# Later transposes of the row maxima, two pairs of heads in turn, and a longer lead of the preparation over the attention

## The chip, the cores and the metric

The kernel runs on one core of one Trainium2 chip. The metric is the device time of one launch in microseconds (us), given as the median of several runs. Five engines of the core matter here: TensorE (PE, with its weight loads PEld), VectorE (DVE), ScalarE (ACT), GpSimd (POOL) and SyncE (SP), whose queue issues nearly all DMAs. The profiles and the traces come from one profiled execution.

## What is computed

One layer of a perceiver: cross attention of 512 queries over a context of 8192 rows (16 heads of 64, that is 8 pairs of heads), then a state space block with its gated network, then a mixture of 16 experts. Only the first part is touched by the change.

```python
def _L0_xattn_ref(Q, K, V, Wq, bq, Wk, bk, Wv, bv, Wo, bo):   # Q: 512 x 512, K = V: 8192 x 512
    q = (scale * (Q @ Wq + bq)).reshape(bs, q_len, NH, DM)      # NH 16, DM 64
    k = (K @ Wk + bk).reshape(bs, kv_len, NH, DM)
    v = (V @ Wv + bv).reshape(bs, kv_len, NH, DM)
    qk = jnp.einsum('nlhd,nshd->nhls', q, k)
    a = jax.nn.softmax(qk, axis=-1)
    o = jnp.einsum('nhls,nshd->nlhd', a, v).reshape(bs, q_len, NH * DM)
    return o @ Wo + bo
...
x = x + _L0_xattn_ref(_layernorm(x), ctx_1024, ctx_1024, ...)
x = x + _L0_attn_ref(_layernorm(x), ...)     # state space block and gated network
x = x + _L0_ffn_ref(_layernorm(x), ...)      # router, 16 experts, shared expert
```

## The kernel before

**Preparation in four passes.** Each of the `NPASS` = 4 passes prepares two pairs of heads. The context is cut into `NCH` = 16 chunks of 512 rows. For each chunk a pass projects K for its two pairs (`kproj_units`, lines L254 to L262) and V (`vproj_units`, two groups, L278 to L285). Each of these four groups fills one PSUM bank, is copied out by ACT (L261, L284), and its rounding error is kept by DVE (L262 `khl`, L285 `vs`), after which the bank is free. The banks come from `bank_j`, two of them while attention runs. A group is cut into four steps; after each the generator yields the nanoseconds that the step is taken to need (648).

**Row maxima as side work.** The softmax needs an upper bound for each row ahead of the attention. `smax_units` multiplies the queries with the chunk's K (L303, into the two banks `psx`), ACT copies the scores out (L308 `sf`), and DVE keeps a running maximum (L316 `runm`). When a pass is through, `maxrow_units` reduces the running maximum of each pair on DVE (two L324 and one L325, the result is `mx`), waits for some steps, transposes it on PE (L329 `ptm`, which takes a bank from `bank_j` as well), copies it on ACT (L331 `mrow`), and sends it by two small DMAs on SP (L333) into row 64 of the tile `qlm`, where the scores of the attention read it.

These generators stand in a list, `side`. The function `pump` takes one step from the first generator in the list. It is called after every second projection step (every fourth in the first pass), and after every one when the list has more than two entries. A step that yields 0 uses up its pump like any other. In the last pass nothing is left to project when the maxima are reduced: the side list is then pumped empty, and the planner counts `LAST / 10` = 800 ns for each of these pumps.

**Attention in 480 + 32 steps.** 16 units (8 pairs, two halves of the queries) have `NSTEP` = 32 steps each. A step has the scores of 256 rows (L367 with `qhh`, L368 with `qlm` and `kb`), exponentials on ACT (L375, and L377 in every even step), the difference of their two precisions on DVE (L379 in odd steps, L380), and the products with V (L397, L400 reads the tile of L380). The products of a step are issued two steps after its scores. At the end of a unit its output is transposed (`unit_end`, L418, also into a bank of `bank_j`).

**The order.** From the second pass on, PE, DVE and ACT work in the order of the program (`manual_schedule`). The planner lets the preparation run ahead by `LEAD` ns of its own counted time, and then spreads the rest evenly over `NFILL` = 378 attention steps: half of a step's share before the products with V, half after them.

```python
rate = ((NPASS - 1) * PASSN + LAST - LEAD) / NFILL
...
    cur = scores(u, m, loads[n // 4], sp, n > NFILL)
    advance(start + LEAD + (n + 0.5) * rate)
    ...
        drain()
    advance(start + LEAD + (n + 1.0) * rate)
```

When a pair's first unit starts (n = 128, 256 and 384 for the first pairs of passes two to four), an assertion in the program wants its maxima to have been issued. The first pass runs alone; its maxima are reduced and transposed within the lead of the second. After the attention of the first 15 units, the last unit and the rest of the layer (`tail`) follow.

Of the kernel before, what the change touches and what calls it, by code (L numbers as in the profile page):

```python
# [41 lines left out]
def perceiver_layer(ctx: ExitStack, tc: tile.TileContext, a: dict, out: bass.AP):  # L42
# [87 lines left out]
    def bank_j(shape, dtype, name):  # L130

        if jn[1]:
            jn[0] += 1
            if jn[0] % 3 == 0:
                return ps_o.tile(shape, dtype, name=name, tag="po1")
        return ps_j.tile(shape, dtype, name=name, tag="pj")
# [34 lines left out]
    def stage_w(src, n, tag, stage=("wst", 1), bufs=2):  # L171
        st = sb2.tile([P, NC4, n], F32, name=f"wst_{tag}", tag=stage[0], bufs=stage[1])
        nc.sync.dma_start(st, src)
        return lambda: split_w(st, n, tag, bufs)
# [8 lines left out]
    def load_w(*x, **k):  # L183
        return stage_w(*x, **k)()
# [4 lines left out]
    def first_norm():  # L189
        xn = sb2.tile([P, 4, DM], F32, name="xn", tag="runm0", bufs=1)  # L190
        layernorm(sb1, xn, x_sb, "ln0")
        transpose_split(xn, xTh, xTl)
        bo_bc = sb2.tile([P, DM], F32, name="bo_bc", tag="t2k", bufs=4)
        nc.sync.dma_start(bo_bc, a["bo"].to_broadcast((P, DM)))
        for i in range(4):
            nc.gpsimd.tensor_tensor(x_sb[:, i, :], x_sb[:, i, :], bo_bc, ALU.add)
# [9 lines left out]
    def qproj(p, w):  # L206
        wh, wl = w
        ps = bank_j([P, NQ], F32, f"psq{p}")
        mm3(ps, lambda i: wh[:, i, :], lambda i: wl[:, i, :], lambda i: xTh[:, i, :], lambda i: xTl[:, i, :], NC4)
        q32 = sb2.tile([P, NQ], F32, name="q32", tag="t2k", bufs=4)  # L210
        nc.scalar.activation(q32, ps, AF.Identity, bias=bq_sb[:, p : p + 1], scale=1.0 / WS)
        qh = sb2.tile([P, NQ], F16, name="qh", bufs=4)
        ql = sb2.tile([P, NQ], F16, name="ql", bufs=2)
        split_dve(qh, ql, q32)
        return qh, ql

    def qplace(p, qh, ql):
        qhh = qhhs[p % NQT]
        qlm = qlms[p % NQT]
        for hh in range(2):  # L220
            s = slice(hh * 64, hh * 64 + 64)
            nc.sync.dma_start(qhh[0:64, hh, :], qh[s])
            nc.sync.dma_start(qhh[64:128, hh, :], qh[s])
            nc.sync.dma_start(qlm[0:64, hh, :], ql[s])
        state[p]["q"] = qhh, qlm

    def ctx_first(c):
        t = []
        for j in (0, 2):
            u = sb3.tile([P, 2, 2, CH], F16, name="ctxc", tag="phl" if c % 2 else "ctxc", bufs=4)  # L230
            t.append(u)
            f = sb2.tile([P, 2, CH], F32, name="cf", tag="p32", bufs=3)
            nc.sync.dma_start(f, a["ctx"][c][:, j : j + 2])
            if j:
                nc.vector.tensor_copy(u[:, 0], f)
            else:
                nc.scalar.copy(u[:, 0], f)  # L237
            nc.vector.tensor_tensor(u[:, 1], f, u[:, 0], ALU.subtract)  # L238
            nc.sync.dma_start(ctx_d[c][:, j // 2], u)
        return t  # L240

    def ctx_load(c):
        t = []
        for j in range(2):
            u = sb3.tile([P, 2, 2, CH], F16, name="ctxc", tag="ctxc", bufs=4)
            nc.sync.dma_start(u, ctx_d[c][:, j])
            t.append(u)
        return t
# [70 lines left out]
    def maxrow_units(p, i, runm):  # L319
        runm = runm[i]  # L320
        qlm = state[p]["q"][1]
        m = sb2.tile([P, 2, 4], F32, name="mx")
        for w in (256, 128):
            nc.vector.tensor_tensor(runm[:, :, :, 0:w], runm[:, :, :, 0:w], runm[:, :, :, w : 2 * w], ALU.max)  # L324
        nc.vector.tensor_reduce(m.rearrange("p h q -> p q h"), runm[:, :, :, 0:128], axis=AX.X, op=ALU.max)  # L325
        for _ in range(3):
            yield 0
        pt = bank_j([P, P], F32, "ptm")
        nc.tensor.transpose(pt[0:8, :], m.rearrange("p h q -> p (h q)"), ident)  # L329
        r = sb2.tile([8, P], F16, name="mrow")  # L330
        nc.scalar.activation(r, pt[0:8, :], AF.Copy, bias=PSHIFT, scale=-1.0)  # L331
        for hh in range(2):
            nc.sync.dma_start(  # L333
                qlm[64:65, hh, :].rearrange("o (a b) -> o a b", b=P), r[hh * 4 : hh * 4 + 4, :]
            )
        state[p]["ready"] = True
        yield 300

    bcount = [0]

# [88 lines left out]
    def filler():  # L429
        side = []  # L430

        def pump():
            while side:
                u = next(side[0], None)
                if u is not None:
                    yield u
                    break
                side.pop(0)

        def pass_weights(g):  # L440
            pr = (2 * g, 2 * g + 1)
            out = []
            for src, n, tag, bufs in (
                (a["Wk"][pr[0]], P, "k", 4), (a["Wk"][pr[1]], P, "k", 4), (a["Wv"][g], 256, "v", 2),
                (a["Wq"][pr[0]], P, "q", 2), (a["Wq"][pr[1]], P, "q", 2),
            ):
                w = stage_w(src, n, tag, bufs=bufs)
                yield None
                out.append(w())
            yield out[0:2], out[2], out[3:5]  # L450

        nw = None
        for g in range(NPASS):
            pr = (2 * g, 2 * g + 1)
            if g == 0:
                wk0 = load_w(a["Wk"][0], P, "k", bufs=4)
                nct = ctx_first(0)
                wk = [wk0, load_w(a["Wk"][1], P, "k", ("p32", 3), bufs=4)]
                wv = load_w(a["Wv"][0], 256, "v", ("p32", 3))
                nc.sync.dma_start(x_sb, a["x"])  # L460
                wq = [load_w(a["Wq"][p], P, "q", ("t2k", 4)) for p in pr]
            else:
                wk, wv, wq = nw
                qh = [qproj(p, w) for p, w in zip(pr, wq)]
                yield 2 * 2592
            runm = [None, None]
            ks = [[None] * NCH for _ in pr]
            for c in range(NCH):
                if c == NCH - 7 and g < NPASS - 1:
                    nws = pass_weights(g + 1)  # L470
                if c >= NCH - 7 and g < NPASS - 1:
                    nw = next(nws, None) or nw
                ct = nct
                nxt = g * NCH + c + 1
                if nxt < NPASS * NCH:
                    nct = ctx_first(nxt) if nxt < NCH else ctx_load(nxt % NCH)
                gens = [kproj_units(p, c, ct, wk[i], ks[i]) for i, p in enumerate(pr)]
                gens += [vproj_units(g, c, ct, wv, j) for j in range(2)]
                k = 0
                for n, gen in enumerate(gens):  # L480
                    for u in gen:
                        yield u
                        k += 1
                        if k % (2 if g else 4) == 0 or len(side) > 2:
                            yield from pump()
                if g == 0 and c == 0:
                    first_norm()
                    qh = [qproj(p, w) for p, w in zip(pr, wq)]
                    yield 2 * 2592
                if c == 2:  # L490
                    for p, q in zip(pr, qh):
                        qplace(p, *q)
                side += [smax_units(c, i, qh[i][0], ks[i][c], runm, g == 0) for i in range(2)]
            side += [maxrow_units(p, i, runm) for i, p in enumerate(pr)]
            if g == NPASS - 1:
                while side:
                    yield from pump()
                    yield LAST / 10
            passes[0] = g + 1

    fill = filler()
    done = [0.0]

# [45 lines left out]

    units = [(p, h) for p in range(NPAIR) for h in range(2)]  # L550
    NLAST = len(units) - 1
    LEAD = 27500
    loads = {}

    def load(j):
# [9 lines left out]
    load(0)  # L565
    advance(start + LEAD)
    load(1)
    pend, enders, early = [], [], weight_prep()
    NFILL = 12 * NSTEP - 6
    rate = ((NPASS - 1) * PASSN + LAST - LEAD) / NFILL  # L570
    sp = (sb2, sb3, 3)
# [12 lines left out]
    for n in range(NLAST * NSTEP):  # L584
        u, m = units[n // NSTEP], n % NSTEP
# [4 lines left out]
        cur = scores(u, m, loads[n // 4], sp, n > NFILL)  # L590
        advance(start + LEAD + (n + 0.5) * rate)
        if enders and m == 4:
            for _ in enders.pop(0):
                pass
        while len(pend) > (2 if m == 2 else 1):
            drain()
        advance(start + LEAD + (n + 1.0) * rate)
        pend.append((u, m, cur))
# [14 lines left out]
    u = units[NLAST]  # L613
# [881 lines left out]
```

## Time and profile before

| what | value |
|---|---|
| median of 3 runs | 2570.77 us (2567.15 to 2572.27) |
| the profiled execution's own time | 2565.43 us |
| its span in the profile | 2563.7 us |
| granted TensorE clock, mean | 0.979 |
| busy: PE / DVE / ACT / POOL | 2361.3 / 2046.2 / 1947.5 / 73.8 us |
| first pass and the lead | to about 293 us |
| attention and preparation together | about 293 to 1592 us |
| attention alone, with the tail's start | about 1592 to 1867 us |
| the eight transposes L329 | 271.7 to 1592.2 us |

A row of the timeline gives the start, the duration, the engine, the line with the operation, what is written from what, and in brackets the idle time of the engine just before it and what ended that. A row of the windows gives the busy time of PE, PEld, DVE, ACT and POOL in a stretch, then the granted clock of PE, the share of the DMA engines and their GB/s. In the view of a tile, the rows under "its engine sat idle before it" tell for how long the engine that was to write the tile had been idle and what ended it.

### The profile page before, as it was taken

The numbers are of one execution on the slowest core, as the hardware profiler recorded it, in microseconds if no ns is written. First come the engines' busy times: TensorE is split into PE (matmuls) and PEld (weight loads), VectorE is DVE, ScalarE is ACT, GpSimd is POOL, SyncE is SP. The second block draws the span as 40 slices with busy tenths as digits, with TensorE's granted clock in tenths as the row PEclk, the third lists the DMA queues.
The fourth block names the chain that finished last, engine by engine and source line by source line (L and its number), as shares of the span: only waits on it lengthen the run. The fifth ranks groups of instructions, "written<-read, shape, count | busy, mean of one in ns | idle before, by whom it ended". The sixth has DMA issues, their size and how long they took to land. (4 is left out here: it accounts for less than half of the span.)

```text
span 2563.7 us, 56681 instructions
## 1 busy us (share of the span) xinstructions
PE 2361.3 (92%) x22958; PEld 1722.3 (67%) x22958; DVE 2046.2 (80%) x2378; ACT 1947.5 (76%) x3734; POOL 73.8 (3%) x77
## 2 busy tenths in 40 slices
PE   7999899999999999999999998998878678899896
PEld 3555577777666777766777776897756456577775
DVE  6776578888888888887888777998899999746685
ACT  5787788888878888877888888997958557434685
POOL 3000000000000000000000000000000000001112
PEclk9999999999999999999999999999999889999998
DMA  7983777787777787777778664777711212388897
GB/s 267 304 272 133 215 213 227 231 238 232 216 231 227 219 247 236 226 213 213 240 216 234 175 171 133 196 207 210 200 59 40 101 50 84 125 281 274 315 360 232
DMA packets 355199, 529.52 MB, mean 207 GB/s; under 512 B 28194, under 2 KB 221922, under 8 KB 354660
## 3 DMA queue, kind: packets, MB, share of 16 engines
q1 hardware_dynamic: 349156, 513.23, 65.7%
q0 software_dynamic: 3616, 8.66, 1.5%
q8 instruction: 182, 2.98, 0.5%
q10 hardware_dynamic: 2160, 3.95, 0.5%
q14 instruction: 85, 0.70, 0.1%
HBM read 396.65 MB, written 126.97 MB: 204 GB/s over the span
## 5 line engine op out<-in xcount | busy, mean ns | idle before, releaser
L380 DVE TENSOR_TENSOR phl<-p,phl 128x1024 f16<-128x1024 f32 x512 | 626.8, 1225 | 191.5 <-ACT phl L377 175.6
L375 ACT ACTIVATE p<-pss 128x512 f32<-128x512 f32 x1024 | 597.6, 622 | 112.1 <-issue 43.5
L308 ACT ACTIVATE sf<-psx 128x512 f16<-128x512 f32 x1024 | 558.6, 625 | 70.2 <-PE psx L303 69.5
L367 PE MATMUL pss<-qhh,k 128*128 128x256 f16 x2048 | 478.3, 274 | 14.1 <-ACT phl L377 11.9
L368 PE MATMUL pss<-qlm,kb 128*128 128x256 f16 x2048 | 477.1, 273 | 0.8 <-DMA v<-v_d 0.7
L316 DVE TENSOR_TENSOR runm<-runm,sf 128x2048 f16<-128x2048 f16 x240 | 292.4, 1220 | 51.4 <-ACT sf L308 51.3
L397 PE MATMUL po<-v,phl 128*128 128x130 f16 x4096 | 322.3, 220 | 3.9 <-DVE oq L410 3.4
L377 ACT ACTIVATE phl<-pss 128x512 f16<-128x512 f32 x512 | 312.8, 611 | 0.0
L397 PEld LDWEIGHTS <-phl 128*128 128x128 f16 x4096 | 270.5, 98 | 61.7 <-issue 15.3
L278 PE MATMUL psv<-wh_v,ctxc 128*128 128x256 f16 x1024 | 283.4, 277 | 7.3 <-ACT wh_v L179 3.2
L279 PE MATMUL psv<-wl_v,ctxc 128*128 128x256 f16 x1024 | 282.0, 275 | 1.1 <-DVE wl_v L180 1.1
L280 PE MATMUL psv<-wh_v,ctxc 128*128 128x256 f16 x1024 | 282.0, 275 | 0.0
L367 PEld LDWEIGHTS <-k 128*128 128x128 f16 x2048 | 200.3, 98 | 65.0 <-issue 20.0
L368 PEld LDWEIGHTS <-kb 128*128 128x128 f16 x2048 | 200.7, 98 | 52.1 <-issue 14.9
L303 PE MATMUL psx<-khl,qh 64*128 64x512 f16 x1024 | 208.1, 386 | 18.2 <-ACT sf L308 13.1
L929 PE MATMUL py<-hs,ident 128*128 128x256 f32 x512 | 141.2, 430 | 76.6 <-DVE hs L926 76.5
L400 PE MATMUL po<-v,phl 128*128 128x65 f16 x4096 | 208.2, 193 | 1.4 <-DVE phl L380 1.4
L254 PE MATMUL psk<-ctxc,wh_k 128*128 128x512 f16 x512 | 197.4, 386 | 10.8 <-ACT ctxc L237 9.0
L379 DVE CAST phl<-p 128x1024 f16<-128x1024 f32 x256 | 176.1, 688 | 30.8 <-ACT p L375 30.6
L255 PE MATMUL psk<-ctxc,wh_k 128*128 128x512 f16 x512 | 196.0, 383 | 0.9 <-DVE ctxc L238 0.9
L256 PE MATMUL psk<-ctxc,wl_k 128*128 128x512 f16 x512 | 195.9, 383 | 0.0
L929 PEld LDWEIGHTS py<-hs,ident 128*128 128x128 f32 x512 | 104.8, 213 | 108.3 <-DVE hs L926 90.9
(315 smaller groups left out, 3814.4 us busy)
## 6 DMA issues: line engine op xcount, KB each, us to landing
v<-v_d SPq DMA_DIRECT2D x128, 520.0 KB
k<-k_d SPq DMA_DIRECT2D x256, 256.0 KB
ctxc<-ctx_d SPq DMA_DIRECT2D x96, 512.0 KB
wef<-in_gu_dram SPq DMA_DIRECT2D x72, 512.0 KB
v_d<-vs SPq DMA_DIRECT2D x128, 260.0 KB
k_d<-khl SPq DMA_DIRECT2D x128, 256.0 KB
kb<-k_d SPq DMA_DIRECT2D x128, 256.0 KB
wpm<-w_d SPq DMA_DIRECT2D x48, 512.0 KB
```

The source lines that it names most:

```text
L278: nc.tensor.matmul(ps[:, t, :], lhsT=ct[i // 2][:, 0, i % 2, sl], rhs=wh[:, i, :], start=i == 0, stop=False)
L279: nc.tensor.matmul(ps[:, t, :], lhsT=ct[i // 2][:, 0, i % 2, sl], rhs=wl[:, i, :], start=False, stop=False)
L280: nc.tensor.matmul(ps[:, t, :], lhsT=ct[i // 2][:, 1, i % 2, sl], rhs=wh[:, i, :], start=False, stop=i == NC4 - 1)
L308: nc.scalar.activation(dst, ps, AF.Copy, scale=1.0 / (8.0 * WS))
L316: nc.vector.tensor_tensor(r, r, sf, ALU.max)
L367: nc.tensor.matmul(ps[:, hh], lhsT=k[:, hh, sl], rhs=qhh[:, hh, qs], start=True, stop=False)
L368: nc.tensor.matmul(ps[:, hh], lhsT=b[:, hh, sl], rhs=qlm[:, hh, qs], start=False, stop=True)
L375: nc.scalar.activation(p32[:, i], pss[i], AF.Exp, scale=sc)
L377: nc.scalar.activation(ph[:, i], pss[i], AF.Exp, scale=sc)
L380: nc.vector.tensor_tensor(pl, p32, ph, ALU.subtract)
L397: nc.tensor.matmul(o, lhsT=ph[:, i, hh, qs], rhs=vv, start=first, stop=False, **kw)
L929: nc.tensor.matmul(py[:, j, :], lhsT=ident, rhs=hs[:, n, 1:], start=k == 0, stop=False)
```

## The change

Three edits. In `maxrow_units` seven steps that yield 0, where there were three, stand between the reduction and the transpose. The two pairs of a pass enter the side list as one generator, `turns`, which takes a step from each of them in turn, where they stood one behind the other. `LEAD` is 36000 where it was 27500, and `rate`, which is worked out from it, goes from 1723.3 to 1700.8 ns for each step.

```diff
@@ maxrow_units
         nc.vector.tensor_reduce(m.rearrange("p h q -> p q h"), runm[:, :, :, 0:128], axis=AX.X, op=ALU.max)
-        for _ in range(3):
+        for _ in range(7):
             yield 0
         pt = bank_j([P, P], F32, "ptm")
@@ new
+    def turns(gens):
+
+        while gens:
+            for g in list(gens):
+                u = next(g, None)
+                if u is None:
+                    gens.remove(g)
+                else:
+                    yield u
@@ filler
-            side += [maxrow_units(p, i, runm) for i, p in enumerate(pr)]
+            side.append(turns([maxrow_units(p, i, runm) for i, p in enumerate(pr)]))
@@ perceiver_layer
-    LEAD = 27500
+    LEAD = 36000
```

## The prediction

> **What bounds the kernel now.** I read the engine shares of the page first, then busy time by stage, then the tile of the transposed maxima, and last the timelines around its eight transposes.
>
> ```profile
> PE 2361.3 (92%) x22958; PEld 1722.3 (67%) x22958; DVE 2046.2 (80%) x2378; ACT 1947.5 (76%) x3734; POOL 73.8 (3%) x77
> ```
>
> ```profile
> 293.00:1578.00 1285.00, 1257.85 (x13105) 911.65 (x13102) 1050.97 (x1250) 1074.08 (x2115) 0.10 (x1) 1.00 0.75 217
> 1578.00:1602.00 24.00, 15.99 (x226) 14.30 (x226) 20.59 (x22) 14.91 (x30) 2.65 (x5) 1.00 0.45 119
> ```
>
> The second fence is busy time by window (PE, PEld, DVE, ACT, POOL; clock; DMA). While attention and preparation run together, PE is busy 98%, so only its 27 us of idle time can be won. In the 24 us in which the last pass drains, PE is busy 67% and DVE 86%: there DVE sets the pace.
>
> ```profile
>   DVE mx L325: 21.4, 7
> ...
>   DVE vs L285: 12.6, 6
> ...
>   ACT mrow L331: 16.6, 8
> ```
>
> This is the tile ptm: what ended the idle time ahead of the transposes (weight load and matmul are both counted), and who waited. Two things hold a transpose: the reduction mx, or the bank it takes, which the DVE correction of an earlier projection (vs, khl) frees. The PE timeline has each stall in its brackets:
>
> ```profile
> 271.68 0.27 PE L329 MATMUL ptm<-ident,mx 128*8 128x128 f32 x1 [3.19 <-DVE khl L262]
> 278.97 0.27 PE L329 MATMUL ptm<-ident,mx 128*8 128x128 f32 x1 [0.77 <-DVE vs L285]
> 708.24 0.27 PE L329 MATMUL ptm<-ident,mx 128*8 128x128 f32 x1 [2.68 <-DVE vs L285]
> 1153.88 0.27 PE L329 MATMUL ptm<-ident,mx 128*8 128x128 f32 x1 [2.40 <-DVE vs L285]
> 1163.62 0.38 PE L329 MATMUL ptm<-ident,mx 128*8 128x128 f32 x1 [3.07 <-DVE mx L325]
> 1585.25 0.27 PE L329 MATMUL ptm<-ident,mx 128*8 128x128 f32 x1 [3.67 <-DVE mx L325]
> 1592.24 0.27 PE L329 MATMUL ptm<-ident,mx 128*8 128x128 f32 x1 [3.57 <-DVE mx L325]
> ```
>
> With 0.26 us at 716.85 that is 19.6 us. The cause is a block of 3.1 us on DVE per pair:
>
> ```profile
> 1580.86 1.22 DVE L380 TENSOR_TENSOR phl<-p,phl 128x1024 f16<-128x1024 f32 x1
> 1582.00 1.94 DVE L324 TENSOR_TENSOR runm<-runm 128x2048 f16<-128x2048 f16 x2
> 1583.98 1.22 DVE L325 TENSOR_REDUCE mx<-runm 128x8 f32<-128x1024 f16 x1
> 1585.11 1.22 DVE L380 TENSOR_TENSOR phl<-p,phl 128x1024 f16<-128x1024 f32 x1
> ```
>
> **A rule weighed: the clock after a stall.** Columns as above; the seventh is the granted clock.
>
> ```profile
> 709.00:713.00 4.00, 4.00 (x22) 2.56 (x20) 3.28 (x6) 1.80 (x3) 0.00 (x0) 0.57 0.51 172
> 1592.30:1596.00 3.70, 3.70 (x54) 3.46 (x55) 2.88 (x3) 2.74 (x6) 0.00 (x0) 1.00 0.08 17
> ```
>
> After the stall of 2.68 us the clock was halved for about 3.4 us (1.7 us lost); after that of 3.57 it stayed full. The windows after 3.19 (0.58) and 3.07 (0.51) show the drop too: three drops, 5.1 us. The Trainium skill, "TensorE: Matmul & The Clock Gate", Part 1 on the clock gate, has the clock halved after an idle window of about 3.4 us and calls that window free-running; its section on oscillation asks for no gaps over that. By its length alone, only the two drain stalls would drop (3.4 us before) and a drain stall after (1.7). I take the trace: three drops before, and after the change a drop at about half of the stalls of 2.7 us or more. The sum below is 6.4 us by the trace and 5.2 by the rule.
>
> **The change part by part.** It adds no arithmetic: the same 16 L324, 8 L325, 8 transposes, 8 copies L331 and 16 DMAs L333 stand in another order. POOL issues none of them. I followed the yields by hand. One pump takes one step from the front of the side list, so two pairs in turn with seven steps each put 14 pumps between a pair's reduction and its transpose, where three were. n is the attention step. Before: reductions at n=118, 121, transposes at 120, 122 (first joint pass); 248, 251 and 250, 252; drain 375, 377 and 376, 378. After: 116, 117 and 122, 123; 247, 248 and 253, 254; 375, 375 and 382, 382. In the alone stage the transposes come at 18.7 and 19.7 us of the planner's time instead of 9.0 and 13.8.
>
> So the cover of a transpose is ample, but two blocks of 3.1 us now follow closely on DVE, and the question is what is late next: corrections that free banks, or L380, which attention needs two steps later. In joint work the way from a score to its use is 2 steps of about 3.3 us plus half the filling, 7.4 us; four exponentials at 0.48 and L380 at 1.15 take 3.4. That leaves 4 us. In the drain two bare steps of 1.58 us leave nearly none.
>
> *Alone stage.* The correction of the second K group ends at 271.62 as now. The V group runs through to 269.6 and the next group needs that bank: wait 2.05. The second reduction pushes the V correction to 275.3, where the group after would start at 274.3: 1.05. The first transpose now falls 0.65 us into a group and needs the bank of the one just ended (about 1.5 us for ACT and DVE): 0.85. Sum 3.95 and 0.3 of clock, against 3.96 and 1.7: gain 1.4 (0 to 3).
>
> *First joint pass.* From the end of the scores of 116: L380 to 3.4, reduction to 6.5, weight preparation 0.7, cast and L380 to 9.0, reduction to 12.1, V correction 12.75. PE wants that bank at 9.95: wait 2.85. The first transpose then stands right between two groups, so the next group waits for exponentials, cast and mrow on ACT: 1.6. With half a clock drop 5.15, against 2.68+0.26+1.7=4.64: loss 0.5 (-2 to +2). The same working for the old order gave 2.45 where 2.68 was measured.
>
> *Second joint pass.* The groups lie differently: the V correction is done at 12.15, PE asks at 12.0, and neither transpose waits. 0.5 with clock, against 2.40+3.07+1.7=7.17: gain 6.7 (3 to 7).
>
> *Drain.* Reductions 1582.0 to 1585.1 and to 1588.2, then L380 of step 376 at 1589.4. PE stands 0.8 for a bank of scores, then 4.35 in that step's second half, then 0.25: 5.4 against 7.24. Steps 380 on run 2.0 earlier. But unit 384 uses the first of these maxima: transpose at 1595.6, behind four exponentials on ACT to 1597.75, mrow 1598.0, two DMAs on SP 1.3 (L333 took 1.21 to 1.34 for two), packets 0.7 to 3 later (seen after these issues): 1600 to 1601.7, where PE is ready at 1597.9. Before, that score waited for its K load until 1601.44. SP's loads for 384 are issued ahead of these DMAs and are not held up. Gain 0.9, half a clock drop 0.85: nothing (-3 to +3).
>
> *Lead.* 27.5 to 36 us takes 22.5 ns off the filling of each of 378 steps and puts 8.5 us ahead of attention. PE had no gap from 279 to 292 and 2% in joint work, so this is time moved; if ACT stood in for PE there, 2% of 8.5 us would be lost. The transposes stay six, three and two steps ahead of their units. The first attention step hits the table load (1.28) with more PE work between the two score maxima: the 2.51 stall at 297.69 becomes about 1.8, gain 0.7.
>
> *Side work later.* Some ten pumps of score maxima are caught up two to a step. Such pairs in an even step cost 0.48 (PE waiting for sf L308 at 614.48, 1035.92); I count three: loss 1.5 (0 to 4). *Unit ends.* The output transposes also take a bank: before, waits of 1.58, 0.55, 1.65 and 1.80 followed them; after, three have the order of the 1.80 one (n=36, 68, 100) and three nearly none: loss 0.4.
>
> Sum: 1.4 - 0.5 + 6.7 + 0 + 0.7 - 1.5 - 0.4 = 6.4 us off the profiled execution's 2565.43 (span 2563.7): 2559.0. That execution is 5.3 below the median 2570.77; off the median, 2564.4.
>
> **The rivals.**
> 1. *The stalls move one for one.* For: DVE has the same 25 us of reductions, and its queue is in order. Against: it was 82% busy in joint work, and the order of the second pass leaves PE covered. If the second pass also waits 4.5 to 5: gain 2, 2569.
> 2. *Slower: the doubled DVE block reaches attention at every pass.* Two reductions, 6.2 us at once, ahead of L380. It decides if the 4 us of slack in joint work are not there (ACT or DVE behind already). Then each of four places costs 6.2 and a clock drop of 1.7, and 384 waits 3 for its row: 34.7 against 24.7 now: 2581. For: the drain shows it. Against: behind a block L380 ended at 1154.96 for the step scored at 1150.44, whose second half ran on PE only at 1164.66.
> 3. *All covered.* The 24.7 us go entirely: 2546. Against: the drain, where DVE is the bound.
> 4. That the change doesn't do what it says: it does more, 14 pumps for seven. That is in the sum.
>
> **How the numbers follow.** A measurement here tells about 0.2% (5.1 us) from no change. Forecast 0.52 (0.40 faster, 0.12 within), rival 1 0.18 (0.13 within, 0.05 slower as the catch-up grows to 4 and the drain costs 3), rival 2 0.18 (0.16 slower, 0.02 within), rival 3 0.12. Faster 0.52, same 0.27, slower 0.21. The bounds added up reach from 15 gained to 6 lost, 2555 to 2577; with the 4 us by which runs lie below their median the range is 2551 to 2577, which leaves out most of rivals 2 and 3.
>
> **What would show it.** Right: the ptm tile with under 3 us of PE stall in all; new waits of 1 to 3 us for khl or vs ahead of L254, L278 near 270, 275 and n=117 to 122; in the drain a wait of 4 to 5 us at L400 for L380; a wait for qlm at 1598 to 1601. Wrong: L380 waits at n=118 or 249 (rival 2), or the same stalls in the second pass (rival 1).

## The result: slower by 0.2%, with the transposes' stalls gone

The changed kernel took 2576.01 us (median of 20 runs, 2568.99 to 2583.08), the kernel before 2571.27 us (20 runs beside it). The ratio is 1.0020, with a 95% interval of 1.0011 to 1.0029. The forecast was 6.4 us faster; it became 4.7 us slower.

The profiled execution of the changed kernel took 2581.91 us, 16.5 more than that of the kernel before, and this is more than the medians differ. Up to the first score of unit 12 (n=384), where every pass has been prepared, it is 7.3 us behind (1607.70 against 1600.44). The other 9.2 us lie behind that point, where the order is the same in both. Over the fourteen profiles this stretch takes between 962.8 and 972.5 us without following the edits (963.3 before, 972.5 after, but 964.0 and 965.0 in e3 and e4, and 970.7 and 971.5 in e5 and e8); its cause is open. What follows explains the part ahead of n=384.

The first fence is the row of engine shares on the page of the changed kernel, the second the busy time by window (columns as in the prediction) in the stages that answer to those shown of before:

```profile
PE 2376.7 (92%) x22958; PEld 1743.7 (68%) x22958; DVE 2048.3 (79%) x2378; ACT 1962.3 (76%) x3734; POOL 69.6 (3%) x77
```

```profile
302.00:1586.00 1284.00, 1251.05 (x13059) 920.87 (x13057) 1047.18 (x1245) 1082.91 (x2104) 0.10 (x1) 1.00 0.74 216
1586.00:1610.00 24.00, 17.93 (x227) 15.35 (x226) 21.65 (x22) 15.11 (x32) 2.65 (x5) 0.93 0.43 113
```

In the joint stage PE is idle for 33 us (1284.00 - 1251.05), where it was 27; in the drain for 6.1 us, where it was 8.0. In the changed kernel the lines behind `turns` have numbers ten higher: L375, L377, L380 and L400 of before are L385, L387, L390 and L410. The tile ptm shows that the transposes are not the reason:

```profile
  DVE khl L262: 2.1, 2
  PE ptm L329: 1.6, 2
...
  ACT mrow L331: 1.6, 2
```

The waits of 21.4 and 12.6 us for mx and vs are gone. The timeline of PE shows what stands in their place (all gaps of 0.9 us or more between 260 and 1610, without those ahead of L303 and the three of 1.80 at unit ends):

```profile
272.13 0.27 PE L278 MATMUL psv<-wh_v,ctxc 128*128 128x256 f16 x1 [1.88 <-DVE khl L262]
275.84 0.38 PE L254 MATMUL psk<-ctxc,wh_k 128*128 128x512 f16 x1 [0.93 <-DVE vs L285]
282.74 0.27 PE L329 MATMUL ptm<-ident,mx 128*8 128x128 f32 x1 [0.91 <-DVE khl L262]
...
713.30 0.38 PE L254 MATMUL psk<-ctxc,wh_k 128*128 128x512 f16 x1 [1.79 <-DVE vs L285]
...
1162.90 0.38 PE L254 MATMUL psk<-ctxc,wh_k 128*128 128x512 f16 x1 [0.99 <-DVE vs L285]
1181.18 0.27 PE L378 MATMUL pss<-qlm,kb 128*128 128x256 f16 x1 [1.65 <-DMA qlm<-mrow]
...
1597.85 0.62 PE L410 MATMUL po<-v,phl 128*128 128x65 f16 x8 [4.22 <-DVE phl L390]
1608.96 0.27 PE L378 MATMUL pss<-qlm,kb 128*128 128x256 f16 x1 [0.99 <-DMA qlm<-mrow]
```

But for the 1.65 us for qlm at 1181.18, these are waits of the kind that the prediction named. With smaller ones of 0.89, 0.38 and 0.27 us they come to 14.9 us where 19.6 went, so a part of the gain is left. The loss is at L303, the scores from which the row maxima are taken. First the group's row on the page of before, then on that of after (busy time, mean ns, idle time just before them):

```profile
L303 PE MATMUL psx<-khl,qh 64*128 64x512 f16 x1024 | 208.1, 386 | 18.2 <-ACT sf L308 13.1
```

```profile
L303 PE MATMUL psx<-khl,qh 64*128 64x512 f16 x1024 | 213.4, 385 | 27.9 <-ACT sf L308 20.4
```

Idle time rises by 9.7 us, and busy time by 5.3 for the same 1024 matmuls, since the second of two matmuls, when it waits for its bank, is counted in the group's span. And the waits recur:

```profile
794.59 0.86 PE L303 MATMUL psx<-khl,qh 64*128 64x512 f16 x2 [0.48 <-ACT sf L308]
848.51 0.86 PE L303 MATMUL psx<-khl,qh 64*128 64x512 f16 x2 [0.49 <-ACT sf L308]
902.96 0.86 PE L303 MATMUL psx<-khl,qh 64*128 64x512 f16 x2 [0.48 <-ACT sf L308]
956.88 0.86 PE L303 MATMUL psx<-khl,qh 64*128 64x512 f16 x2 [0.48 <-ACT sf L308]
```

They lie 54 us apart, that is 16 attention steps or two chunks of the preparation, through most of a pass. Elsewhere such a pair of matmuls takes 0.39 us with no gap ahead of it; here it takes 0.86 after a gap of 0.48. That is about 0.95 us each, or 1.03 by the count of the table below. Before, away from the maxima of a pass, such rows are few; beside these three there are two, at 1377.01 and 1431.15:

```profile
614.48 0.86 PE L303 MATMUL psx<-khl,qh 64*128 64x512 f16 x2 [0.49 <-ACT sf L308]
1035.92 0.86 PE L303 MATMUL psx<-khl,qh 64*128 64x512 f16 x2 [0.48 <-ACT sf L308]
1090.43 0.86 PE L303 MATMUL psx<-khl,qh 64*128 64x512 f16 x2 [0.49 <-ACT sf L308]
```

In the changed kernel, what PE waits for is on ACT at that time:

```profile
846.87 0.61 ACT L385 ACTIVATE p<-pss 128x512 f32<-128x512 f32 x1
847.34 0.62 ACT L387 ACTIVATE phl<-pss 128x512 f16<-128x512 f32 x1
847.82 2.18 ACT L308 ACTIVATE sf<-psx 128x512 f16<-128x512 f32 x4
```

ACT is through with the last of the step's four exponentials at about 847.9 and then copies four score banks in a row. Two pairs of scores came in one step with four exponentials, and there are two banks for them.

### The profile page after: what moved, and what is told of

Read it like the earlier page. It is cut to its first block, busy times and chain, and to the rows that moved or that the text cites. A ratio compares the mean times of both kernels' runs of the same rounds, so it can differ in the third digit from the quotient of the medians.

```text
span 2580.2 us, 56647 instructions
## 1 busy us (share of the span) xinstructions
PE 2376.7 (92%) x22958; PEld 1743.7 (68%) x22958; DVE 2048.3 (79%) x2378; ACT 1962.3 (76%) x3734; POOL 69.6 (3%) x77
## 5 line engine op out<-in xcount | busy, mean ns | idle before, releaser
L390 DVE TENSOR_TENSOR phl<-p,phl 128x1024 f16<-128x1024 f32 x512 | 626.3, 1225 | 186.1 <-ACT phl L387 167.3
L385 ACT ACTIVATE p<-pss 128x512 f32<-128x512 f32 x1024 | 593.9, 614 | 96.7 <-PE pss L378 58.8
L377 PE MATMUL pss<-qhh,k 128*128 128x256 f16 x2048 | 480.5, 275 | 13.8 <-ACT phl L387 10.4
L387 ACT ACTIVATE phl<-pss 128x512 f16<-128x512 f32 x512 | 312.4, 610 | 0.0
L377 PEld LDWEIGHTS <-k 128*128 128x128 f16 x2048 | 200.9, 98 | 71.4 <-issue 24.5
L303 PE MATMUL psx<-khl,qh 64*128 64x512 f16 x1024 | 213.4, 385 | 27.9 <-ACT sf L308 20.4
L410 PE MATMUL po<-v,phl 128*128 128x65 f16 x4096 | 208.3, 193 | 6.2 <-DVE phl L390 6.2
L939 PE MATMUL py<-hs,ident 128*128 128x256 f32 x512 | 149.0, 448 | 68.9 <-DVE hs L936 68.8
L939 PEld LDWEIGHTS py<-hs,ident 128*128 128x128 f32 x512 | 110.7, 224 | 103.0 <-DVE hs L936 81.5
## 6 DMA issues: line engine op xcount, KB each, us to landing
k<-k_d SPq DMA_DIRECT2D x256, 256.0 KB
k_d<-khl SPq DMA_DIRECT2D x128, 256.0 KB
kb<-k_d SPq DMA_DIRECT2D x128, 256.0 KB
```

The costliest lines, as they stand in the source:

```text
L377: nc.tensor.matmul(ps[:, hh], lhsT=k[:, hh, sl], rhs=qhh[:, hh, qs], start=True, stop=False)
L385: nc.scalar.activation(p32[:, i], pss[i], AF.Exp, scale=sc)
L387: nc.scalar.activation(ph[:, i], pss[i], AF.Exp, scale=sc)
L390: nc.vector.tensor_tensor(pl, p32, ph, ALU.subtract)
L939: nc.tensor.matmul(py[:, j, :], lhsT=ident, rhs=hs[:, n, 1:], start=k == 0, stop=False)
```

## The theory and its rivals

**Spacing (P).** A chunk counts 16x648+8x406 = 13616 ns for the planner. At LEAD 36000 the rate is 1700.8, so a chunk lasts 8.006 attention steps. At every second border between chunks two score maxima come one projection step apart instead of two, because an exhausted entry still counts when the side list is taken to be long (`len(side) > 2`). With 8.006 steps to a chunk this close pair falls at the same place for whole passes, and at LEAD 36000 that place is an even step, which has four exponentials, in the second and third of the three joint passes (n=142, 158 and so on; an odd step, n=11 to 91, in the first). At 27500 a chunk has 7.90 steps, and the pairs wander. By hand, 14 even steps hold two score maxima before and 22 after.

**Rivals.** The seven steps and turns delay the side work, and catching up costs (S, B). Or a longer lead costs, or helps, by itself (L).

The waits of all runs stand in one table. Each interval between two matmuls on PE, from the first projection of the second pass to the first score of n=384, is compared with the lower quartile of the intervals between the same two neighbours over all fourteen profiles; what lies above is added up for the matmul that came late. Intervals at the halved clock are added up apart. "All" is the length of this stretch in the one profiled execution. Even in order the columns are not zero (9.2 us for L400 and L397 before). The expectations below count fewer of the waits at L303 (16.6 us before and about 31 after), so only their differences can be set beside this column. The ratio is to the kernel before in the same session.

| run | even steps with two | all, us | L303 for sf | transposes | projections for banks | products with V | half clock | ratio |
|---|---|---|---|---|---|---|---|---|
| before | 14 | 1343.5 | 25.1 | 20.2 | 9.2 | 9.2 | 4.9 | 1 |
| after | 22 | 1350.3 | 41.8 | 1.1 | 15.9 | 13.2 | 1.5 | 1.0020 |
| e1: lead 36000 only | 19 | 1350.8 | 31.2 | 21.3 | 8.3 | 9.0 | 4.6 | 1.0011 |
| e2: steps, turns, lead 27500 | 15 | 1349.9 | 33.3 | 1.1 | 15.2 | 14.0 | 6.6 | 1.0015 |
| e3: after, lead 39000 | 8 | 1342.7 | 24.6 | 1.1 | 17.3 | 13.9 | 8.4 | 0.9985 |
| e4: after, one step later | 13 | 1343.0 | 30.6 | 1.7 | 19.2 | 12.5 | 3.5 | 0.9990 |
| e5: after, border | 10 | 1334.1 | 24.3 | 1.1 | 17.3 | 12.9 | 2.6 | 0.9945 |
| e6: before, lead 39000 | 8 | 1328.3 | 19.3 | 14.3 | 4.1 | 9.5 | 5.0 | 0.9920 |
| e7: e8, last pass in line | 7 | 1331.0 | 21.1 | 1.1 | 15.6 | 13.6 | 3.3 | 0.9905 |
| e8: after, 39000, border | 7 | 1331.8 | 21.1 | 1.1 | 15.6 | 13.8 | 3.9 | 0.9929 |
| e9: three, in line, 39000, border | 5 | 1322.8 | 15.6 | 14.7 | 4.1 | 9.3 | 3.3 | 0.9895 |
| e10: seven, in line, 39000, border | 11 | 1329.0 | 25.5 | 1.9 | 8.4 | 13.4 | 2.6 | 0.9912 |
| e11: three, in turn, 39000, border | 6 | 1323.4 | 17.4 | 4.9 | 8.1 | 13.1 | 3.4 | 0.9899 |
| e12: before, lead 42000 | 15 | 1346.4 | 27.0 | 19.9 | 8.1 | 9.2 | 6.0 | 1.0000 |

After less before: L303 +16.7, transposes -19.1, projections +6.7, products with V +4.0, half clock -3.4, waits for qlm +1.8 (not in the table), the rest 0.1: +6.8. By the same count the doubled even steps cost 1.2 us each after (26.5 us in 22), the doubled odd ones 0.6 (7.7 in 13).

## The experiments

### e1 and e2: the lead alone, the steps alone

e1 is the kernel before, e2 the changed kernel, each with one line edited.

```diff
-    LEAD = 27500
+    LEAD = 36000
```

> The kernel before, with LEAD 36000 alone (three steps, pairs one behind the other). Theory of the step (P): at LEAD 36000 a chunk of the preparation lasts 13616/1700.8 = 8.006 attention steps, so the two score maxima that stand close together at each chunk's border fall at the same place for whole passes, in a step with four exponentials. Followed by hand, 19 even steps have two score maxima in them, 14 before. The waits of PE for sf at L303 go from 16.6 us to about 21 to 25, the stalls of the eight transposes stay near 19 us: 2576 (2573 to 2581). Rival (S): the seven steps and the turns cause the waits, the lead is harmless: 2571, L303 waits 16 to 18 us.

Measured: 2573.77 us, ratio 1.0011 (1.0001 to 1.0021). L303 rose by 6.1 us and the transposes kept their stalls, as P expected; the time is 2.6 above the 2571.2 of before. So the lead alone costs, by little more than the noise.

```diff
-    LEAD = 36000
+    LEAD = 27500
```

> The changed kernel with LEAD put back to 27500 (seven steps and turns stay). P: 15 even steps with two score maxima, waits for sf at L303 about 18 us instead of 31; stalls of the transposes gone as in the changed kernel, but the rows for n=256 come only one step ahead, with a wait for qlm of 3 to 5 us there: 2566 (2562 to 2569). S: no better than the changed kernel, 2576.

Measured: 2574.85 us, ratio 1.0015 (1.0003 to 1.0026). P missed by 9 us. L303 stood at 33.3 us, 8.2 above before, though the even steps are nearly as many (15 and 14). So the seven steps and the turns have a cost at L303 of their own, beside the spacing at borders: the side work that comes later is caught up two to a step, and the larger waits at n=1, 130 and 258 (1.7 to 1.9 us each) stand at the start and in the steps after the maxima. S was right for this half. The wait for qlm at n=256 was 4.29 us, as expected. With the halved clock left out, the stretch of the table is 7.6 us longer in e1 than before, 4.7 in e2 and 10.2 in the changed kernel: both parts of the change cost.

### e3 and e4: the same kernel at another place of the pattern

e3 has LEAD 39000. e4 keeps the rate of the changed kernel and starts the attention one step later:

```diff
-    LEAD = 36000
+    LEAD = 37701
...
-    rate = ((NPASS - 1) * PASSN + LAST - LEAD) / NFILL
+    rate = ((NPASS - 1) * PASSN + LAST - 36000) / NFILL
```

> The changed kernel with LEAD 39000 (rate 1692.9, 8.04 steps to a chunk). P: by hand 8 even and 23 odd steps with two score maxima, where 36000 has 22 and 13. L303 waits about 15 to 18 us less than the changed kernel's 31: 2562 (2558 to 2566). S, and a rival (L) in which a longer lead costs by itself: 2576 to 2580.

> The changed kernel with the rate kept at 1700.8 and the lead longer by one attention step (37701): the same locked pattern, moved from even to odd steps. P: 13 even steps with two score maxima instead of 22, L303 waits down by 7 to 10 us: 2568 (2564 to 2571). L: 2577 or more. A resonance that costs in every phase: 2576.

Measured: e3 2567.37 us, ratio 0.9985 (0.9974 to 0.9996), L303 17.2 us below the changed kernel. e4 2569.19 us, ratio 0.9990 (0.9980 to 1.0000), L303 11.2 below. Both leads are longer than 36000 and both kernels are faster than at 36000, so a longer lead does not cost by itself. e4 has the same rate and the same locked pattern, moved by one step: from even to odd in the second and third joint pass, from odd to even in the first. So the parity of the step makes the difference. e3 missed its number by 5 us; in its profile banks and half clock took more than in the changed kernel (17.3 and 8.4 us), but that profiled execution (2563.93 us) lies 3.4 below the median, so the miss is explained only in part.

### e5: no close pairs at the borders

```diff
-                        if k % (2 if g else 4) == 0 or len(side) > 2:
+                        if k % (2 if g else 4) == 0 or len(side) > (2 if c < 4 else 3):
```

> The changed kernel (LEAD 36000) in which, from the fifth chunk of a pass on, an exhausted entry at the front of the side list no longer makes the list count as long: no pair of score maxima stands close together at a chunk's border. By hand 10 even steps with two score maxima instead of 22. P (close pairs in steps with four exponentials cost 0.8 to 1.7 us each): L303 waits 12 us lower than the changed kernel's, 2564 (2560 to 2568). Rival (B): the waits come from the side work that is behind after the maxima of a pass (chunks 1 to 3), which this leaves alone: 2575.

Measured: 2560.23 us, ratio 0.9945 (0.9928 to 0.9961), at the lead of 36000. L303 fell by 17.5 us, which is all that it had risen by, and the recurring waits are gone. The catching up (chunks 1 to 3) was left alone, and its waits stayed (0.48 to 1.03 us at n=127, 128, 134, 256, 266). The kernel before had close pairs too: its waits at n=63, 79, 94, 201, 216, 232, 314 and 330, all places that lie at borders, add up to 7.7 us. So of the rise of 16.7 us at L303 about 10 are the borders (17.5 less 7.7) and about 7 are other places, those that rival B named and the lead. This agrees with e1 and e2, which rose by 6.1 and 8.2. The edit acts in the first pass as well: the first projection of the second pass starts at 250.8 to 256.0 us in the six profiles that have it, and at 255.1 to 257.9 in the eight that do not (medians 252.7 and 257.4). So between 4 and 5 us of what every kernel with this edit gains over before have nothing to do with L303 in the joint passes. The row of L303 on its page, and on that of e9, to set beside 213.4 and 27.9:

```profile
L303 PE MATMUL psx<-khl,qh 64*128 64x512 f16 x1024 | 204.5, 384 | 16.4 <-ACT sf L308 11.5
```

```profile
L303 PE MATMUL psx<-khl,qh 64*128 64x512 f16 x1024 | 202.0, 385 | 11.5 <-ACT sf L308 8.0
```

### e6 and e12: the kernel before at two longer leads

Only `LEAD` is edited, to 39000 and to 42000.

> The kernel before with LEAD 39000 alone. P: 8 even steps with two score maxima against 14 at 27500: L303 waits 4 to 7 us lower, the transposes' stalls stay near 20: 2565 (2562 to 2569). L (a longer lead costs by itself): 2574 or more, as the run with 36000 alone might have been read.

> The kernel before with LEAD 42000 alone. P: 15 even steps with two score maxima, as at 27500 (14), while 39000 has 8: 2567 (2560 to 2572), clearly above the 2553 of 39000. Rival: a longer lead is what helped at 39000: 2553 or less.

Measured: e6 2552.95 us, ratio 0.9920 (0.9905 to 0.9936); e12 2570.50 us, ratio 1.0000 (0.9989 to 1.0011). So 27500, 36000, 39000 and 42000 give 1, 1.0011, 0.9920 and 1.0000: it is the place in the pattern, not the length. e6 missed its number by 12 us: it gained three times what P expected. L303 gave 5.8 us as foreseen, but the transposes gave 5.9 and the projections 5.1 too: their waits changed with the place as well. That part of e6 was not foreseen, and of its mechanism only the sums in the table are shown.

### e8 and e7: the drain

e8 is the changed kernel with LEAD 39000 and the border edit. e7 has the pairs of the last pass one behind the other:

```diff
-            side.append(turns([maxrow_units(p, i, runm) for i, p in enumerate(pr)]))
+            mrs = [maxrow_units(p, i, runm) for i, p in enumerate(pr)]
+            side += mrs if g == NPASS - 1 else [turns(mrs)]
```

> The changed kernel with LEAD 39000 and no close pairs at borders. By hand 7 even and 11 odd steps with two score maxima (8 and 23 without the border edit). P: L303 waits a little below those at 39000 alone: 2564 (2560 to 2567). If odd pairs cost as much as even ones: 2558.

> The changed kernel with LEAD 39000, no close pairs at borders, and in the last pass the two pairs one behind the other again (seven steps stay). Against the next run this tells what the double block on DVE costs in the drain: the wait of 4.2 us at L410 for L390 is split into two of at most 2, and the first pair's row is issued four steps earlier, so the waits for qlm at n=384 (1.3 us) go: 3 us below the next run, 2560. Rival: the two blocks cost as much apart as together: equal to the next run.

Measured: e8 2556.00 us, ratio 0.9929 (0.9915 to 0.9943), e7 2548.82 us, ratio 0.9905 (0.9888 to 0.9921). e8 came in 8 us below its number, and why stays open. Ahead of L410, e8 waits 4.22 us once, e7 1.11 and 2.35, and the waits of 0.99 and 0.27 for qlm at n=384 are gone: 2.0 us, where about 3 were expected. From n=376 to n=416 the traces differ by 4.1 us; in e8 the clock was also halved for 6.8 us in this stretch (from 1575.3), in e7 not. The medians differ by 7, more than the drain explains, but the intervals of the ratios overlap.

The double block can be read off the timeline of DVE in the drain of the changed kernel:

```profile
1590.35 1.94 DVE L324 TENSOR_TENSOR runm<-runm 128x2048 f16<-128x2048 f16 x2
1592.32 1.22 DVE L325 TENSOR_REDUCE mx<-runm 128x8 f32<-128x1024 f16 x1
1593.46 1.94 DVE L324 TENSOR_TENSOR runm<-runm 128x2048 f16<-128x2048 f16 x2
1595.44 1.22 DVE L325 TENSOR_REDUCE mx<-runm 128x8 f32<-128x1024 f16 x1
1596.57 1.22 DVE L390 TENSOR_TENSOR phl<-p,phl 128x1024 f16<-128x1024 f32 x1
```

From 1590.35 to 1596.57 nothing else runs on DVE, and L390 comes behind it.

### e9, e10, e11: three or seven steps, in line or in turn

With e8 these are the four combinations at LEAD 39000 and the border edit, where the spacing is nearly repaired. Against e8, e9 has neither edit of the change, e10 only the seven steps, e11 only the turns:

```diff
-        for _ in range(7):
+        for _ in range(3):
...
-            side.append(turns([maxrow_units(p, i, runm) for i, p in enumerate(pr)]))
+            side += [maxrow_units(p, i, runm) for i, p in enumerate(pr)]
```

> Three steps, pairs one behind the other, LEAD 39000, no close pairs at borders: the kernel before with lead and border alone. With the run of seven steps and turns under the same lead and border, and the next two, this is a table of two by two in which the spacing of the score maxima is nearly the same (5 to 11 even steps with two). P: transposes' stalls about 14 as at 39000 alone, L303 waits 15 to 18: 2550 (2546 to 2553), that is 5 or more below seven steps with turns (2556). Rival (T): seven steps and turns are a gain once the spacing is repaired: 2560 here.

> Seven steps, pairs one behind the other, LEAD 39000, no close pairs at borders. If the loss of seven steps with turns is the double block on DVE (waits for banks and for L390), then one block at a time with seven steps keeps the transposes' stalls near 1 and has fewer of those waits: 2547 (2543 to 2551), the best of the four. If the loss is in the side work that comes later, it stays: 2555.

> Three steps, pairs in turn (seven pumps between a reduction and its transpose), LEAD 39000, no close pairs at borders. Double block, but side work less late: double block theory 2555 (waits for banks 12 to 16, L410 for L390 4); late side work theory 2550.

Measured: e9 2541.67 us, ratio 0.9895 (0.9877 to 0.9912); e11 2544.19, 0.9899 (0.9881 to 0.9916); e10 2547.81, 0.9912 (0.9896 to 0.9927); e8, 0.9929. The intervals of neighbours overlap, but e9 and e10 ran side by side, and all four runs of e10 (2547.37 to 2551.11) lie above the four of e9 (2540.98 to 2546.80). The table ranks the four the same way. e9 and e11 came in below all numbers expected for them, e9 by 8 us, of which the first pass (e5) is about half. e9 has 14.7 us at the transposes and is still the fastest. e10 saves 12.8 there, and pays 9.9 at L303, 4.3 for banks and 4.1 at the products with V. By the second column the seven steps cost 6.2 us in line (e9 to e10) and 8.4 in turn (e11 to e8), and the turns 0.6 with three steps (e9 to e11) and 2.8 with seven (e10 to e8). So most of the loss comes with the seven steps, which delay the side work; the double block by itself costs little. The theory of the double block expected e10 to be the best and e11 to lose; e10 had its number right (2547) but is not the best, and e11 nearly equals e9.

e9 is the fastest version that was run, 1.05% below the kernel before. It is the old order of the maxima with another lead and the border edit.

## Why the prediction was wrong

The sum had seven terms. Five of them held, and the sum failed in the two on the lead and on the side work. These two gave 0.8 us of loss at L303 together (0.7 gained, 1.5 lost), and the table has 16.7. So the miss is 15.9 us at L303. From the gain of 6.4 that was forecast to the loss of 6.8 in the table it is 13.2 in all, since the rest came out 2.7 better than forecast.

- **Alone stage (forecast 2.05, 1.05, 0.85):** measured 1.88, 0.93, 0.91, and no clock drop. Right.
- **First joint pass (2.85 and 1.6):** 1.79 and, at 725.10 for mrow on ACT, 0.89. Right in kind and place, too large.
- **Second joint pass (done at 12.15, wanted at 12.0):** 0.99 for a bank, and 1.65 for qlm at n=256, which was not foreseen. "The transposes stay six, three and two steps ahead of their units" was true, but three steps were not enough. The rows stood behind another DMA on SP, which waited for vs on DVE (start, duration):

```profile
1174.78 0.33 SPq L287 DMA_DIRECT2D v_d<-vs  x1
1175.19 2.66 SPq L333 DMA_DIRECT2D qlm<-mrow  x4
```

  ACT had the first row ready at 1173.78. SP issued it only behind the store of vs, 1.4 us later, and the scores waited until 1181.18. From the issue to this release it took 6.0 us, while the prediction, for the drain, had counted 1.3 and then 0.7 to 3. The prediction had looked at SP's loads and not at its stores.
- **Drain (0.8, 4.35, 0.25, then a row at 1600 to 1601.7):** 0.38, 4.22 and a wait of 0.99 and 0.27 for qlm. Right in the large. The transposes' 7.24 us became 5.86, and one drop of the clock came with them (3.4 us at half, from 1597.6).
- **Unit ends (three of the kind of 1.80):** 1.80 at 428.63, 537.34 and 646.97. Right.
- **Lead ("time moved", 0; with its table load +0.7):** this is where it failed. The prediction worked out that 22.5 ns of filling leave each step and did not ask what that does to the places where side work meets attention. The 0.7 did not come either: the stall of 2.51 went, but 0.47 and 0.38 at L377 and 1.19 at L303 stand in the first steps instead. In e1 the lead alone cost 2.6 us. e4 shows that the place alone is worth 11.2 us at L303, and e5 that 17.5 us go when the close pairs go.
- **Side work later (three doubled steps at 0.48, loss 1.5):** mis-sized twice. A doubled even step mostly costs 1.03 us and up to 1.78, because half of the wait is hidden in the group's busy time. And doubled even steps went from 14 to 22, most of the new ones at the borders, a place that the prediction did not look at. Together with the lead, this term measured 16.7 us at L303.

Neither rival fits. Rival 1 (stalls that move one for one, 2569) is 7 us too low, and the stalls shrank instead of moving. Rival 2 (2581) put the price of the double block on every pass; PE waited for L390 in the drain alone, and the 4 us of slack in joint work were there. The signs that the prediction set for being right came (the wait for qlm later, at 1608.96), and none of those for being wrong: all of them looked at the transposes, the banks and L380, and none at L303. That 2576.01 lies in the range of 2551 to 2577 is luck: the side work had a bound of 4 us and L303 took 16.7, and what covers the difference are the bounds of terms that held and the allowance for noise. Two slips in its sums change nothing: four exponentials at 0.48 and L380 at 1.15 make 3.07 and not 3.4, and half a clock drop stands at 0.7 in the first joint pass and at 0.85 in the drain.

On the clock, the trace and the rule differed by 1.2 us in the sum, so the choice decided nothing. In the changed kernel the one drop between 262 and 1600 us came at the one stall above 3.4 us (4.22), as the rule has it; before, the three drops came at 2.68, 3.07 and 3.19 and none at 3.57 and 3.67, against it. Half clock fell by 3.4 us in the table, about what was forecast.

## What to carry to other kernels

Where two streams are interleaved by counted time, the ratio of their periods is a quantity to check: near a whole number, a bad meeting of two instructions is repeated for a whole stage, and any edit to a lead or a cost moves it. Write down which side step falls beside which attention step over several periods before reading anything into a lead, and test an edit to the order at more than one lead. Hiding a visible stall gains only what is left after the delayed work has been paid for at its new place, so price the catching up, with the busy time of a group as well as the idle time ahead of it.

## What the runs showed of the hardware

PE gaps and the halved clock were compared in all fourteen profiles between 262 and 1600 us. A drop of about 3.4 us began within 2.5 us of 3 of 46 gaps of 1.4 to 2 us, of 8 of 19 between 2 and 2.6, of 8 of 13 between 2.6 and 3.5, and of 12 of 14 above that. Here the longer gaps had a drop more often, and no length decided it. Four drops of the 35 had no such gap beside them, and three lasted 6.8 us. The fourteen kernels share many of their gaps, so the counts are not independent.
